# A graph layer and an LSTM on one core: residual additions moved to VectorE, the comparison moved ahead, preparation reordered

## The chip, the core and the metric

The kernel runs on one core of a Trainium2 chip. Its engines are TensorE (PE in the profile; its weight loads are PEld), VectorE (DVE), ScalarE (ACT), GpSimd (POOL) and SyncE (SP), which only issues transfers. The metric is the device time of one execution in microseconds. Three timed runs of the kernel took 1111.95, 1112.99 and 1113.43 us; the median is 1112.99.

## The reference

x has 1250 rows of 512 numbers; 20000 edges (src, dst) join rows, sorted by dst. Two residual layers follow each other:

```python
x = x + gnn(layernorm(x), src, dst, ...)
x = x + lstm(layernorm(x))          # one sequence of 1250 steps, state of 512
```

The graph part computes h = feat @ fc_w.T + fc_b, the degree of each row, and twice a sum over neighbours, a product with a 512x512 matrix w1, a product of h with a matrix w2, a bias and relu. The LSTM computes four gates from x_t and the state before, for 1250 steps, and its output h_t is added to x.

## The kernel before, in words

**Rows.** The 1250 rows are cut into P = 32 stretches of LEN = 40 rows. A tile has 128 rows (four of each stretch), and there are T = 10 tiles.

**Preparation** (lines 282 to 516). The edges are counted into a dense adjacency with matmuls: VectorE makes two one-hot matrices for each group of 125 edges (`make_onehot`, L401 and L403), PE multiplies them (L414, L417). Groups go in batches of four; 40 batches; eight buffers, so one-hots are made two batches ahead, and batch n + 2 is made when batch n has been multiplied. Beside that, for every tile t: `stats` (L153, L154) and `scales` (L158, L88 to L95, L339) give mean and scale of the first layer norm; `normed` (ACT, L429) normalises; `transposed` turns the tile on PE (L165) and copies it out on ACT (L170); `product` (PE, L176) multiplies by fcT; VectorE adds the bias (L488); the result is turned again, and two products with w2 follow, whose sums get their biases on VectorE (L463). fcT is made from fc_w by 16 transposes (`turn_fcw`, L377, copied out by L379). `with_identity` scales w2 on ACT (L181) and adds a diagonal on VectorE (L184).

The order on PE, VectorE and ACT is written out by hand (`manual_schedule`, L326): every engine runs its instructions in the order in which the program names them. A loop over slots s = 0 to 12 (L465) sets it. `per_slot` (L457) gives how many batches of edges are counted at three places of a slot, for s = 0, 1, 2, 3: (0,0,0), (1,1,0), (1,1,1), (1,2,1). In slot s, tile s is turned, tile s - 1 multiplied by fcT, h of tile s - 2 turned, and from slot 3 on tile s - 3 multiplied by the two w2. Statistics stand in slot 0 for tiles 1 to 3, in slot 1 for tiles 4 to 6, in slot 2 for tiles 7 to 9, each time right behind the turning of a tile; those of tile 0 stand ahead of the loop, inside the arithmetic on the edges (L383 to L389).

SP issues the loads, in this order: src, tile 0 of x (two transfers), fc_w as one transfer of 1 MiB (L300), tiles 1 to 3 (six), a bias, tiles 4 to 9 (eight), both w2, two biases, and ten fills with zeros of scratch space in HBM (L322). ACT issues dst and x's last rows. GpSimd makes the zeros (L320): 12 partitions of 6144 bf16 elements each.

**Graph layers** (L731 to L772): the sums over neighbours are matmuls with the adjacency (L750). The change doesn't touch them.

**LSTM** (`lstm`, L859). All 32 stretches run at once. Each starts WARM = 84 steps (and 12 more with fewer terms) ahead of its own rows, so that its state has settled by then; step n runs from -84 to 39, and steps 0 to 39 give output. Steps -84 to -63 also compute what the gates get from x. In a step, PE opens the gates from fetched data (L596) and adds 64 matmuls with the state (L604); then, for each half s, `cell` (L608) runs: ACT L611, L613, L615; VectorE L617, L618; ACT L620; VectorE L621, which writes hh (three buffers), and L622, which turns hh into the next state hT. In steps 0 to 39 GpSimd adds hh to the rows x2c (L1032), and after steps 7, 15, 23, 31, 37 and 39 `store` writes rows out. All stores but the last are issued by SP; the last has eight transfers, four on SP, two on ACT and two on GpSimd.

**Comparison.** `keep_state` copies the state before step 0 into snap (L890, L891) and the state after step 39 into last. If the warm-up was long enough, the end state of a stretch equals the state at the start of the next one. Five VectorE instructions and one matmul (L1039 to L1047) count the entries that differ; every engine loads the count (L1048), and if it isn't zero, a slow sequential version runs (L1050 to L1059).

Of the kernel before, what the change touches and what calls it, by code (L numbers as in the profile page):

```python
# [38 lines left out]
def gnn_lstm_kernel(  # L39
# [23 lines left out]
    nc = tc.nc  # L63
# [4 lines left out]
    R = 4 * P  # L68
# [91 lines left out]

    def transpose_in(ps, rows):

        p = ps.tile([128, KD, R], F32, name="psT")
        for k in range(KD):
            nc.tensor.transpose(p[:, k, :], rows[:, k * 128:(k + 1) * 128], ident)  # L165
        return p
# [37 lines left out]
    with ExitStack() as gnn_stack:  # L204
# [77 lines left out]
        with tc.tile_pool(name="prep", bufs=1) as prep, \  # L282
# [16 lines left out]
            fcw = prep.tile([128, KD, D], F32, name="fcw")  # L299
            nc.sync.dma_start(fcw, fc_w.rearrange("(a p) i -> p a i", p=128))  # L300
            biases = [prep.tile([R, D], F32, name=name) for name in ("fcb", "b1", "b2")]
# [16 lines left out]

            zeros = planes.rearrange("b t i d -> b (t i d)")[:4 * EARLY, :12 * G]
            nc.gpsimd.memset(zeros, 0.0)  # L320
            for v in xp_d:
                nc.sync.dma_start(  # L322
                    bass.AP(tensor=v.tensor, offset=v.offset,
                            ap=[[12 * G, 4 * EARLY], [1, 12 * G]]), zeros)

            with tc.manual_schedule(engines={mybir.EngineType.PE, mybir.EngineType.DVE,  # L326
# [6 lines left out]
                def stats(t0, t1):  # L333
                    for t in range(t0, t1):
                        layernorm_stats(work, mv, t, xt[:, t, :])

                def scales(t0, t1):
                    layernorm_scale(prep, mv[:, t0:t1, :], rstd[:, t0:t1], f"ln{t0}")
                    nc.vector.scalar_tensor_tensor(nmr[:, t0:t1], mv[:, t0:t1, 0], -1.0,  # L339
                                                   rstd[:, t0:t1], op0=OP.mult, op1=OP.mult)  # L340


                ends = []
                for name, rows in rows_i:
# [8 lines left out]
                    ends.append(e.rearrange("p i c -> p (i c)"))  # L353
                e_src, e_dst = ends
                none = edges.tile([ER, BW * T], F16, name="none")
                nc.vector.memset(none, 0.0)
# [14 lines left out]

                fcT = prep.tile([128, KD, D], F32, name="fcT")

                def turn_fcw(k):
                    p = psM.tile([128, D], F32, name="psM")
                    for a in range(KD):
                        nc.tensor.transpose(p[:, a * 128:(a + 1) * 128],  # L377
                                            fcw[:, a, k * 128:(k + 1) * 128], ident)
                    nc.scalar.copy(fcT[:, k, :], p)  # L379

                turn_fcw(0)
                turn_fcw(1)
                np_src, o_src = neg_floor_div(e_src, LEN, "stretch")  # L383
                stats(0, 1)
                scales(0, 1)
                turn_fcw(2)
                na_src, q_src = neg_floor_div(o_src, 4, "tile")
# [35 lines left out]

                xns, xTs, hTs, ps_h, ps_b = {}, {}, {}, {}, {}

                def normed(t):
                    if t < T:
                        xns[t] = work.tile([R, D], F32, name="xn")
                        nc.scalar.activation(xns[t], xt[:, t, :], AF.Identity,  # L429
                                             bias=nmr[:, t:t + 1], scale=rstd[:, t:t + 1])  # L430

                BATCH = 4
# [17 lines left out]

                normed(0)
                onehots(0)
                onehots(1)
                turn_fcw(3)

# [9 lines left out]
                for s in range(T + 3):  # L465
                    c0, c1, c2 = per_slot[s] if s < len(per_slot) else (0, 0, 0)
                    if 0 < s < 3:

                        ps_h[s - 1] = product(psM, xTs.pop(s - 1), fcT)
                        count(c0)  # L470
                    if s < T:
                        xTs[s] = transposed(work, psT, xns.pop(s), "xT")
                    if s < 3:
                        t0, t1 = ((1, 4), (4, 7), (7, T))[s]
                        stats(t0, t1)
                        scales(t0, t1)
                    normed(s + 1)
# [9 lines left out]
                    if 0 <= s - 1 < T:  # L487
                        nc.vector.tensor_add(h[:, s - 1, :], ps_h.pop(s - 1), fcb)  # L488
                    count(c2)
                    if s == 2:  # L490
                        for l in range(2):
                            with_identity(w2[l], ALPHA * betas[l], ALPHA * (1.0 - betas[l]))
# [335 lines left out]
        def store(x2c, n0, n1):  # L828

            def rows(j, p0, p1, m):  # L830
                (nc.sync, nc.scalar, nc.gpsimd, nc.sync)[j if n1 == LEN else 0].dma_start(
                    bass.AP(tensor=out.tensor, offset=out.offset + (LEN * p0 + n0) * D + 128 * j,
                            ap=[[LEN * D, p1 - p0], [D, m - n0], [1, 128]]),
                    x2c[32 * j + p0:32 * j + p1, n0:m, :])
# [24 lines left out]
        def lstm(first_yT, Wx, bx, Wh, wh_parts, close_wx):  # L859
# [6 lines left out]

            TOL = 2.0 ** -18
            first = -(WARM + BEFORE) % LEN // 4
# [6 lines left out]
            with ExitStack() as pools:  # L875
# [9 lines left out]
                    "b (n x y) -> b n x y", n=3, x=8)  # L885
                snap, last, apart = held[:, 0], held[:, 1], held[:, 2, :, :31]

                def keep_state(dst, hT):
# [87 lines left out]
                with tc.manual_schedule(engines={mybir.EngineType.PE, mybir.EngineType.DVE,  # L976
# [33 lines left out]
                    for n in range(-WARM, LEN):  # L1010
                        u = AHEAD + WARM + n
                        if n == 0:
                            keep_state(snap, hT)
                        if u == len(units):
                            load_x2c()
# [13 lines left out]
                        if u < len(units):  # L1029
                            put(u, 2)  # L1030
                        if n >= 0:
                            nc.gpsimd.tensor_add(x2c[:, n, :], x2c[:, n, :], hh)  # L1032
                            if n + 1 in stores:
                                store(x2c, ([0] + stores)[stores.index(n + 1)], n + 1)
                    keep_state(last, hT)

                nc.vector.tensor_sub(apart, last[:, :, 0:31], snap[:, :, 1:32])  # L1039
                nc.vector.scalar_tensor_tensor(apart, apart, -1.0, apart, op0=OP.mult, op1=OP.max)  # L1040
                nc.vector.tensor_scalar(apart, apart, TOL, None, OP.is_le)
                near = seq.tile([128, 1], F32, name="near")
                nc.vector.tensor_reduce(near, apart, mybir.AxisListType.XY, OP.add)
                pc = ps_c.tile([R, G], F32, name="pc")[:1, :1]
                nc.tensor.matmul(pc, near, ones, start=True, stop=True)
                far = seq.tile([1, 1], I32, name="far")
                nc.vector.tensor_scalar(far, pc, -1.0, float(128 * 8 * 31), OP.mult, OP.add)  # L1047
                n_far = nc.values_load(far, min_val=0, max_val=128 * 8 * 31)  # L1048
# [66 lines left out]
```

## Time and profile before

| what | us |
|---|---|
| median of three runs | 1112.99 |
| the profiled execution | 1113.26 |
| its span, first to last instruction | 1111.5 |
| PE busy in the span | 1007.0 |
| VectorE busy | 516.4 |
| ACT busy | 342.8 |
| GpSimd busy | 81.9 |
| start of the matmuls over neighbours (end of the preparation) | 195.2 |
| start of step 0 (first matmul of L604) | 917.3 |
| last state written | 1100.8 |

Times within the execution are counted from the start of the span. The profile's views used here are: the page; the chain of waits, which follows the work that ended last back through what released it; the timeline, which gives instructions in order of time with start, length, engine, line, names, shape and, in brackets, the idle time ahead and what ended it; and the table of stretches, which gives each engine's busy time and PE's granted clock (1.00 is full speed) in chosen intervals.

### The profile page before, as it was taken

The numbers are of one execution on the slowest core, as the hardware profiler recorded it, in microseconds if no ns is written. First come the engines' busy times: TensorE is split into PE (matmuls) and PEld (weight loads), VectorE is DVE, ScalarE is ACT, GpSimd is POOL, SyncE is SP. The second block draws the span as 40 slices with busy tenths as digits, with TensorE's granted clock in tenths as the row PEclk, the third lists the DMA queues.
The fourth block names the chain that finished last, engine by engine and source line by source line (L and its number), as shares of the span: only waits on it lengthen the run. The fifth ranks groups of instructions, "written<-read, shape, count | busy, mean of one in ns | idle before, by whom it ended". The sixth has DMA issues, their size and how long they took to land.

```text
span 1111.5 us, 26611 instructions
## 1 busy us (share of the span) xinstructions
PE 1007.0 (91%) x10972; PEld 517.7 (47%) x10972; DVE 516.4 (46%) x1753; ACT 342.8 (31%) x1267; POOL 81.9 (7%) x138
## 2 busy tenths in 40 slices
PE   4899999999999998999999988888888888888884
PEld 2455454554455443344444444444444444444442
DVE  7767667102400665655544544444444444444443
ACT  2322125203401024443333333333333333333332
POOL 2000000100000011111001170000000000011001
PEclk9899999999999999999999999999999999999998
DMA  7500000600200037662323393332233333334431
GB/s 217 79 1 1 1 1 35 234 1 18 74 1 1 0 113 230 205 184 82 109 85 114 101 231 97 97 90 87 88 89 99 88 88 87 107 77 116 119 78 20
DMA packets 37271, 98.51 MB, mean 89 GB/s; under 512 B 5711, under 2 KB 10680, under 8 KB 37018
## 3 DMA queue, kind: packets, MB, share of 16 engines
q1 hardware_dynamic: 27280, 68.67, 23.1%
q0 software_dynamic: 7232, 23.63, 6.2%
q10 hardware_dynamic: 2625, 4.39, 1.3%
q8 instruction: 89, 1.46, 0.5%
q14 instruction: 45, 0.36, 0.1%
HBM read 74.29 MB, written 19.76 MB: 85 GB/s over the span
## 4 chain that ended last, share of the span: by engine, by line
PE 49%; issue 26%; DVE 13%; ACT 7%; DMA 1%; SPq 1%; POOL 1%; DVEq 0%; ACTq 0%; POOLq 0%
PE gates L604 29%; PE psM L919 8%; PE psM L176 8%; DVE adj L617 3%; ACT adj L620 3%; DVE hT L622 2%; DVE cg L618 2%; DVE adj L621 2%; ACT cg L611 2%; PE acc L417 2%; ACT adj L613 2%; DVE od L403 1%; DMA fcw<-in_L_gnn_fc_w_dram 1%; POOL xp_d L939 1%; PE gates L596 1%
## 5 line engine op out<-in xcount | busy, mean ns | idle before, releaser
L604 PE MATMUL gates<-Wh,hT 128*32 128x256 f32 x7936 | 457.5, 381 | 61.4 <-DVE hT L622 61.3
L604 PEld LDWEIGHTS gates<-Wh,hT 128*32 128x32 f32 x7936 | 233.4, 109 | 257.1 <-DVE hT L622 122.9
L617 DVE TENSOR_TENSOR adj<-adj,cg 128x128 f32<-128x128 f32 x248 | 68.2, 275 | 231.7 <-ACT adj L613 231.5
L919 PE MATMUL psM<-Wx,xT 128*128 128x512 f32 x320 | 147.6, 607 | 0.5 <-DVE adj L929 0.5
L750 PE MATMUL agg<-adj,planes 128*128 128x512 bf16 x720 | 130.1, 344 | 1.9 <-DVE x L463 1.9
L611 ACT ACTIVATE cg<-gates 128x64 f32<-128x64 f32 x248 | 55.4, 224 | 213.6 <-PE gates L604 210.1
L620 ACT ACTIVATE adj<-cg 128x64 f32<-128x64 f32 x248 | 63.6, 256 | 131.7 <-DVE cg L618 131.7
L750 PEld LDWEIGHTS <-planes 128*128 128x128 bf16 x720 | 70.4, 98 | 62.4 <-DVE x L463 2.7
L621 DVE TENSOR_TENSOR adj<-adj 128x64 f32<-128x64 f32 x248 | 55.9, 225 | 82.5 <-ACT adj L620 82.5
L919 PEld LDWEIGHTS psM<-Wx,xT 128*128 128x128 f32 x320 | 58.7, 192 | 71.3 <-issue 69.0
L622 DVE STREAM_TRANSPOSE hT<-adj 128x64 f32<-128x64 f32 x248 | 60.9, 245 | 24.2 <-DVE adj L621 1.4
L613 ACT ACTIVATE adj<-gates 128x128 f32<-128x128 f32 x248 | 67.2, 271 | 0.1
L618 DVE TENSOR_TENSOR cg<-adj 128x64 f32<-128x64 f32 x248 | 55.8, 225 | 8.5
L939 POOL DMA_DIRECT2D xp_d<-planes x40 | 28.8, 719 | 408.4 <-issue 214.2
L176 PE MATMUL psM<-w,hT 128*128 128x512 f32 x128 | 58.6, 610 | 0.0
L615 ACT ACTIVATE adj<-gates 128x64 f32<-128x64 f32 x248 | 57.0, 230 | 0.0
L403 DVE TENSOR_SCALAR od<-ids,key 125x820 f16<-125x820 f16 (+42 forms) x160 | 55.6, 347 | 0.0
L596 PE MATMUL gates<-h,sel 96*32 96x256 bf16 x992 | 50.0, 273 | 0.0
L1032 POOL TENSOR_TENSOR base<-base,adj 128x128 f32<-128x128 f32 x40 | 18.4, 459 | 414.9 <-DVE adj L621 414.9
L417 PE MATMUL acc<-od,ob 125*128 125x400 f16 (+22 forms) x360 | 46.4, 259 | 0.4
L401 DVE TENSOR_SCALAR ob<-ids,low 125x128 f16<-125x128 f16 x160 | 39.6, 247 | 15.5 <-PE acc L417 15.4
L931 ACT CAST planes<-adj 128x512 bf16<-128x512 f32 x40 | 24.7, 618 | 60.8 <-DVE adj L929 60.7
(163 smaller groups left out, 722.3 us busy)
## 6 DMA issues: line engine op xcount, KB each, us to landing
h<-xp_d SPq DMA_DIRECT2D x136, 384.0 KB
xp_d<-planes POOLq DMA_DIRECT2D x40, 384.0 KB, 3.1
base<-x POOLq DMA_DIRECT2D x40, 64.0 KB, 4.5
w<-in_L_gnn_w_dram SPq DMA_DIRECT2D x2, 1024.0 KB
w<-in_L_gnn_w_dram POOLq DMA_DIRECT2D x2, 1024.0 KB, 5.9
xp_d<-planes SPq DMA_DIRECT2D x10, 144.0 KB
h<-in_x_dram SPq DMA_DIRECT2D x10, 128.0 KB
h<-in_x_dram SPq DMA_DIRECT2D x10, 120.0 KB
```

Source lines behind the costliest of these rows:

```text
L176: nc.tensor.matmul(p, lT[:, k, :], rhs[:, k, :], start=(k == 0), stop=(k == KD - 1))
L417: nc.tensor.matmul(blocks[i][:, (d0 - i * BW) * T:(d1 - i * BW) * T], ob, od[:, (d0 - lo) * T:(d1 - lo) * T], start=False, stop=last)
L604: nc.tensor.matmul(ps[s][32 * j:32 * (j + 1), :, :], hT[b // 2][:, b % 2, :], Wh[:, b, :, 128 * j + 64 * s:128 * j + 64 * (s + 1)], start= ...
L611: nc.scalar.activation(cg[:, 1, :], p[:, 3, :], AF.Tanh)
L613: nc.scalar.activation(sg, p[:, 0:2, :], AF.Sigmoid)
L617: nc.vector.tensor_mul(pr, sg, cg)
L618: nc.vector.tensor_add(cg[:, 0, :], pr[:, 0, :], pr[:, 1, :])
L620: nc.scalar.activation(th, cg[:, 0, :], AF.Tanh)
L621: nc.vector.tensor_mul(hh[:, m], so, th)
L622: nc.vector.transpose(hT.rearrange("p b c -> p (b c)"), hh[:, m])
L750: nc.tensor.matmul(p[:, :n * R], planes[:, k, pl, f * 128:(f + 1) * 128], adj[:, k, t0:t0 + n, :].rearrange("b i r -> b (i r)"), start=(k ...
L919: nc.tensor.matmul(p, yT[n][:, k, :], quarter(Wx[:, k, :, :], j), start=(k == 0), stop=(k == KD - 1))
```

## The change

It does six things:

1. The zeros in SBUF are 96 partitions of 768 elements instead of 12 of 6144. The HBM area filled is the same.
2. fc_w is loaded in four transfers of 128 rows, and `turn_fcw(a)` turns one such block instead of one block of columns.
3. The first tile's statistics, normalisation and turning, and the first two blocks of fc_w, stand ahead of the arithmetic on the edges; the other two blocks stand behind the first one-hots.
4. The statistics of tiles 4 to 6 move from slot 1 to the end of slot 2's counting, those of tiles 7 to 9 from slot 2 to slot 5.
5. The addition of hh moves from GpSimd to VectorE, behind the step's second cell. The last store's eight transfers are issued by SP and ACT in turn.
6. Both states are kept CHECK = 3 steps earlier (before step -3 and before step 37); the comparison runs on VectorE at the start of step 37, its matmul behind the cells of step 37. Where the count is loaded stays.

```diff
-    def transpose_in(ps, rows):
-        p = ps.tile([128, KD, R], F32, name="psT")
+    def transpose_in(ps, rows, name="psT"):
+        p = ps.tile([128, KD, R], F32, name=name)
...
-            nc.sync.dma_start(fcw, fc_w.rearrange("(a p) i -> p a i", p=128))
+            for a in range(KD):
+                nc.sync.dma_start(fcw[:, a, :], fc_w[a * 128:(a + 1) * 128, :])
...
-            zeros = planes.rearrange("b t i d -> b (t i d)")[:4 * EARLY, :12 * G]
+            W = 768
+            zeros = planes.rearrange("b t i d -> b (t i d)")[:4 * EARLY * 12 * G // W, :W]
             nc.gpsimd.memset(zeros, 0.0)
             for v in xp_d:
                 nc.sync.dma_start(
                     bass.AP(tensor=v.tensor, offset=v.offset,
-                            ap=[[12 * G, 4 * EARLY], [1, 12 * G]]), zeros)
+                            ap=[[W, 4 * EARLY * 12 * G // W], [1, W]]), zeros)
...
+                def turn_fcw(a):
+                    p = transpose_in(psM, fcw[:, a, :], "psM")
+                    nc.scalar.copy(fcT[:, :, a * 128:(a + 1) * 128], p)
...
                 e_src, e_dst = ends
+                stats(0, 1)
+                scales(0, 1)
+                turn_fcw(0)
+                normed(0)
+                turn_fcw(1)
+                xTs[0] = transposed(work, psT, xns.pop(0), "xT")
                 none = edges.tile([ER, BW * T], F16, name="none")
...
-                def turn_fcw(k):
-                    p = psM.tile([128, D], F32, name="psM")
-                    for a in range(KD):
-                        nc.tensor.transpose(p[:, a * 128:(a + 1) * 128],
-                                            fcw[:, a, k * 128:(k + 1) * 128], ident)
-                    nc.scalar.copy(fcT[:, k, :], p)
-                turn_fcw(0)
-                turn_fcw(1)
                 np_src, o_src = neg_floor_div(e_src, LEN, "stretch")
-                stats(0, 1)
-                scales(0, 1)
-                turn_fcw(2)
                 na_src, q_src = neg_floor_div(o_src, 4, "tile")
...
-                normed(0)
                 onehots(0)
                 onehots(1)
+                turn_fcw(2)
                 turn_fcw(3)
...
-                    if s < T:
+                    if 0 < s < T:
                         xTs[s] = transposed(work, psT, xns.pop(s), "xT")
-                    if s < 3:
-                        t0, t1 = ((1, 4), (4, 7), (7, T))[s]
-                        stats(t0, t1)
-                        scales(t0, t1)
+                    if s == 0:
+                        stats(1, 4)
+                        scales(1, 4)
                     normed(s + 1)
...
                     count(c2)
+                    if s in (2, 5):
+                        stats(s + 2, s + 5)
+                        scales(s + 2, s + 5)
                     if s == 2:
                         for l in range(2):
                             with_identity(w2[l], ALPHA * betas[l], ALPHA * (1.0 - betas[l]))
...
-                (nc.sync, nc.scalar, nc.gpsimd, nc.sync)[j if n1 == LEN else 0].dma_start(
+                (nc.scalar if n1 == LEN and j % 2 else nc.sync).dma_start(
...
-            TOL = 2.0 ** -18
+            TOL, CHECK = 2.0 ** -18, 3
...
+                def compare():
+                    nc.vector.tensor_sub(apart, last[:, :, 0:31], snap[:, :, 1:32])
+                    nc.vector.scalar_tensor_tensor(apart, apart, -1.0, apart,
+                                                   op0=OP.mult, op1=OP.max)
+                    nc.vector.tensor_scalar(apart, apart, TOL, None, OP.is_le)
+                    nc.vector.tensor_reduce(near, apart, mybir.AxisListType.XY, OP.add)
+
+                def count_apart():
+                    pc = ps_c.tile([R, G], F32, name="pc")[:1, :1]
+                    nc.tensor.matmul(pc, near, ones, start=True, stop=True)
+                    nc.vector.tensor_scalar(far, pc, -1.0, float(128 * 8 * 31), OP.mult, OP.add)
...
-                        if n == 0:
+                        if n == -CHECK:
                             keep_state(snap, hT)
+                        if n == LEN - CHECK:
+                            keep_state(last, hT)
+                            compare()
...
                         if u < len(units):
                             put(u, 2)
+                        if n == LEN - CHECK:
+                            count_apart()
                         if n >= 0:
-                            nc.gpsimd.tensor_add(x2c[:, n, :], x2c[:, n, :], hh)
+                            nc.vector.tensor_add(x2c[:, n, :], x2c[:, n, :], hh)
                             if n + 1 in stores:
                                 store(x2c, ([0] + stores)[stores.index(n + 1)], n + 1)
-                    keep_state(last, hT)
-                nc.vector.tensor_sub(apart, last[:, :, 0:31], snap[:, :, 1:32])
...
```

More of the change, by code (lines that the diff above doesn't have):

```diff
@@ L340, in scales, with normed @@
                                                    rstd[:, t0:t1], op0=OP.mult, op1=OP.mult)
+                xns, xTs, hTs, ps_h, ps_b = {}, {}, {}, {}, {}
+                def normed(t):
+                    if t < T:
+                        xns[t] = work.tile([R, D], F32, name="xn")
+                        nc.scalar.activation(xns[t], xt[:, t, :], AF.Identity,
+                                             bias=nmr[:, t:t + 1], scale=rstd[:, t:t + 1])
+                fcT = prep.tile([128, KD, D], F32, name="fcT")
+                def turn_fcw(a):
+                    p = transpose_in(psM, fcw[:, a, :], "psM")
+                    nc.scalar.copy(fcT[:, :, a * 128:(a + 1) * 128], p)
                 ends = []
@@ L370, in neg_floor_div @@
                     return q, r
-                fcT = prep.tile([128, KD, D], F32, name="fcT")
-                def turn_fcw(k):
-                    p = psM.tile([128, D], F32, name="psM")
-                    for a in range(KD):
-                        nc.tensor.transpose(p[:, a * 128:(a + 1) * 128],
-                                            fcw[:, a, k * 128:(k + 1) * 128], ident)
-                    nc.scalar.copy(fcT[:, k, :], p)
-                turn_fcw(0)
-                turn_fcw(1)
                 np_src, o_src = neg_floor_div(e_src, LEN, "stretch")
-                stats(0, 1)
-                scales(0, 1)
-                turn_fcw(2)
                 na_src, q_src = neg_floor_div(o_src, 4, "tile")
@@ L422, in count_group @@
                     return done
[L424 to L430, printed above, removed]
                 BATCH = 4
@@ L886, in lstm @@
                 snap, last, apart = held[:, 0], held[:, 1], held[:, 2, :, :31]
+                near = seq.tile([128, 1], F32, name="near")
+                far = seq.tile([1, 1], I32, name="far")
+                def compare():
[8 more added lines that the diff above has]
+                    nc.vector.tensor_scalar(far, pc, -1.0, float(128 * 8 * 31), OP.mult, OP.add)
                 def keep_state(dst, hT):
@@ L1030, in lstm @@
                             put(u, 2)
+                        if n == LEN - CHECK:
+                            count_apart()
                         if n >= 0:
-                            nc.gpsimd.tensor_add(x2c[:, n, :], x2c[:, n, :], hh)
+                            nc.vector.tensor_add(x2c[:, n, :], x2c[:, n, :], hh)
                             if n + 1 in stores:
                                 store(x2c, ([0] + stores)[stores.index(n + 1)], n + 1)
-                    keep_state(last, hT)
[L1039 to L1047, printed above, removed]
                 n_far = nc.values_load(far, min_val=0, max_val=128 * 8 * 31)
```

## The prediction

> **What bounds the kernel now.** I read the profile's own time first, then the chain of waits, then the timeline of its two ends. The profiled execution took 1113.26 us, its span 1111.5, so 1.8 lie outside the span; the three timed runs have their median at 1112.99, 0.3 lower. All sums below are made against 1113.3. The chain has three stretches that the change touches: the preparation (0 to 195 us), the 40 output steps (917 to 1101) and the tail (1101 to 1111.5).
>
> In the preparation the timeline shows VectorE held back at the start:
> ```profile
> 2.01 5.21 POOL L320 MEMSET planes<- 12x6144 bf16 x1
> 3.18 4.19 DVE L346 CAST src_f<-src_i 80x250 f32<-80x250 int32 x1 [2.29 <-DMA src_i<-in_src_dram]
> ...
> 8.46 0.28 DVE L346 CAST dst_f<-dst_i 80x250 f32<-80x250 int32 x1
> ```
> The two casts have one shape; the first takes 4.19 us, not 0.28, and ends at 7.37, just after GpSimd's memset (7.22). The table by stretches (columns: length, busy PE, PEld, DVE, ACT, POOL with counts, granted clock, DMA share, GB/s), cut where the clock changes, shows what PE does afterwards:
> ```profile
> 31.36:34.78 3.42, 1.09 (x8) 0.67 (x8) 3.32 (x13) 0.00 (x0) 0.00 (x0) 1.00 0.80 83
> 34.78:38.19 3.41, 1.99 (x9) 1.56 (x10) 2.93 (x17) 3.13 (x4) 0.00 (x0) 0.50 0.66 68
> 38.19:41.61 3.42, 3.42 (x5) 1.34 (x5) 3.42 (x20) 3.09 (x4) 0.00 (x0) 0.50 0.82 87
> 41.61:45.02 3.41, 3.35 (x26) 2.06 (x26) 2.60 (x16) 0.81 (x2) 0.00 (x0) 1.00 0.67 72
> ```
> VectorE is busy nearly throughout, PE waits for it, and after the idle stretch PE's clock is half for 6.8 us. From 45 to 100 us PE is then busy without a gap, and the chain follows it: a gain before 45 us is carried to the end, one behind it is not.
>
> In the output steps, the chain of waits at a step without GpSimd's add and at one with it:
> ```profile
> 911.88 0.27 ACT adj L620
> 912.15 0.03 issue
> 912.17 0.24 DVE adj L621
> ```
> ```profile
> 961.69 0.27 ACT adj L620
> 961.95 0.03 issue
> 961.98 0.02 DVEq L621
> 962.00 0.04 issue
> 962.05 0.24 DVE adj L621
> ```
> L621 writes hh. With the add, VectorE's queue takes one wait more in front of it, some 0.07 us, and that is the whole difference of the two steps.
>
> In the tail the chain is VectorE alone, and the store to HBM lies beside it (second fence, timeline):
> ```profile
> 1101.46 0.43 DVE S L1039
> 1101.89 0.02 issue
> 1101.91 0.43 DVE S L1040
> ...
> 1103.38 0.14 DVE far L1047
> ```
> ```profile
> 1101.02 1.72 SPq L831 DMA_DIRECT2D out_dram<-base  x4
> ```
> The last state is done at 1100.81, far at 1103.52, and the span ends at 1111.46: 7.9 us of register loads, barriers and one long GpSimd drain (4.56 us from 1106.06 in the instruction records).
>
> **Steps without GpSimd.** Step starts in the chain: 908.34, 912.80, 917.26 (4.46 apart), then 930.98, 935.51, 940.04 (4.53). The longer period begins at step 3, where the hh buffer read by GpSimd in step 0 is written again (three buffers). With the reader on VectorE that wait has nothing to wait for: 37 steps (3 to 39) by 0.07 is **-2.6 us**. From step 23 the period is 4.55 to 4.61, which I can't tie to the add; from 930.98 to 1094.98 the 36 steps take 164.0 us, at 4.46 they would take 160.6, so 3.4 is the upper end and 2.0 the lower. The add itself, 128x128 on two operands, has its like in L617 (0.275 us); it stands behind the step's last transpose, and VectorE is then idle 1.70 us before the next L617. That idle time hides it; without it, 40 additions would cost 12 us. Stores don't hold it: GpSimd's add of the step after a store (959.15) follows the one before (954.63) by 4.52, as elsewhere.
>
> **Comparison ahead.** Off the tail go two pairs of L890/L891 (1100.81 to 1101.43), L1039 to L1043, the matmul and L1047: 1100.81 to 1103.52, 2.7 us. They go to step 37, behind the add of step 36: add 0.28, states 0.62, comparison 1.64 (0.43, 0.43, 0.30, 0.42 and gaps) make 2.54 us in the 1.70 of idle time, so L617 and with it the step are late by **+0.85** (bounds 0.6 to 1.2). The first snapshot (0.62) fits its idle time at step -3 as it does at step 0. The one-column matmul stands on PE behind gates that are done, and far (0.14) behind the second cell: nothing. What is late in the tail then is the store. VectorE's add ends near 1101.1, SP issues four transfers in 1.72 us, ACT now four as well (its two took 0.38 and 0.70), to about 1103.0; load of the register and branch took SP 0.9 more. Against 1104.4 now that is 1103.9: **-0.5**. Unknown is GpSimd's drain. It has no stores any more (its two were issued up to 1102.4). If the drain belongs to them, all of it can go, and SP's own last waits (1106.8 now) set the end, up to 4.4 less. No other drain of the trace resembles it (0.19 us at the start). I take the drain as fixed, because it ends 8 us after the last of those issues while their median landing is 1.8 us, and keep 4.4 for the range.
>
> **Short fill.** 768 elements a partition for 6144: by proportion 0.65 us, between the 0.2 of a 128-element memset and the 5.21. Up to 1.17 us it is over before the cast starts (3.18). The cast then takes 0.28: 3.9 us earlier for VectorE's whole queue. The ten transfers of zeros stand last on SP and nothing waits for them until the 440s: nothing.
>
> **Order of the preparation.** VectorE ends dst_e at 9.87 now, at 6.0 afterwards. First statistics and scales run from 11.94 to 15.33 now, of which the square root spends 0.94 behind an fcT copy on ACT; it now stands ahead of those copies: 2.5 us, to 8.5. Then ids 0.58, divisions 1.51 and 2.11, one-hots of two batches 2.39, to 15.1, and statistics 1 to 3, 4.2 us, to 19.3, where 24.0 is now. Following that: xn 0.81, transpose 0.65, copy 0.59, second product at 21.5 (26.26 now), to 25.0.
>
> Here the second statistics (25.17 to 29.21 now) are gone, and what is late next is PE: batch 2 is counted after that product, and frees the one-hot buffers at 25.3. VectorE idles from 22.3, then makes one-hots 4 to 6 and a sum (4.5 us, to 29.8), and now does statistics 4 to 6 there (4.1, to 33.9). Their square root stands on ACT ahead of the scaling of both w2 (3.7 us, so 32.9 to 36.6), VectorE's diagonal additions end at 37.5, one-hots 7 and 8 at 38.9 and 40.3. PE has finished its third product and batch 6 at 32.3 and waits 5.5 us. So the first pair of w2 products starts at 40.5; the timeline has it at 45.15: -4.65. But PE's idle time now spans a full stretch of 3.4 us directly ahead of those products. The row above prices it: busy 32% of a stretch, the next at half clock. I take one half-clock stretch in front of full work, +1.7: **-3.0** net. Bounds: two stretches and a late third product, 0; no stretch, -5.
>
> The third statistics move from 32.33 to the end of slot 5. There 7.1 us of w2 products follow on PE without VectorE, and VectorE idles 2.6 and 2.1 us per slot waiting for PE; 4.1 us are covered, nothing. Were that cover gone, 4.1.
>
> **fc weight in four blocks.** Three issues more by 0.51 us on SP, 1.5 us for the rows and weights queued behind. The fifth row transfer now waits from 6.6 to 11.45 for the whole weight; with blocks that wait is for one block and should be no longer. A block's landing isn't shown; the nearest rows are x's first two transfers (124 KB each, issued 1.2 to 2.9, landed by about 5 by the bytes moved) and the whole weight (issued 2.99, landed 11.45). At either end the first product can start by 12.7 (weights 11.45, transposes, copy), and the second product waits for VectorE until 21.5: nothing, either way. The Trainium skill speaks against this part: DMA: Bandwidth & Descriptors, section Bandwidth, asks for transfers of 1 MiB and more, as smaller ones spend their time on fixed costs. By its 341 GB/s for 1 MiB the weight would be there in 3.1 us; the trace needed 8.5 beside the rows, and either way the first product isn't what VectorE's chain waits for.
>
> On the half clock: the Trainium skill's TensorE: Matmul & The Clock Gate, Part 1, says that an idle window of about 3.4 us halves the clock until a busy one has passed. Here windows of 32% and 39% sufficed (stretch from 14.3); by the rule read strictly a window would have to be empty, and the +1.7 might fall away.
>
> **Sum.** -3.0 - 2.6 + 0.85 - 0.5 = -5.25: **1108.0 us**.
>
> **Rivals.**
> 1. The drain goes with the stores: a further -4.4, 1103.6. For it: GpSimd then issues nothing behind the 650s. Against: 8 us between issue and end of the drain. 22%.
> 2. The front gives nothing: PE's 5.5 us of waiting in slot 3 cost two half-clock stretches and the third product falls into another. 1113.3 - 2.25 = 1111.0. For it: the statistics are put where no w2 products cover them. 15%.
> 3. The change doesn't remove the wait of the steps (VectorE needs one for its own reader): 1108.0 + 2.6 = 1110.6. Against: in the steps before 0, L622 reads hh on VectorE and there is no such wait. 4%.
> 4. Slower: the rows of x for tiles 1 to 3 land late. SP issues them behind three more transfers, and one of them waits for a block; VectorE, in order, stands still at statistics 1. I need them at 15.1. It decides from 22.6 on (7.5 us later eat the 5.25 and 0.2% of the time); landing at 26 gives 1119, at 23.5 about 1116. Against it: now they are issued by 13.2 in spite of the wait for the whole weight. 7%.
>
> The forecast's own case has 52%, 1105.5 to 1110.3.
>
> **Numbers.** A measurement tells about 0.2% (2.2 us) from no change. Faster by more: the forecast's case, rival 1, under half of 2 (6%), half of 3: 82%. Within: 11%. Slower: 7%. The range from 1101.5 (rival 1 with the steps at 3.4 and some of the front's 5) to 1111.5 (rival 2) leaves out rival 4, and some 5% on either side.
>
> **What would show it.** First cast near 0.28 us and statistics 1 to 3 ended near 19.3; first w2 product near 40.5 with a half-clock stretch about it; period 4.46 in steps 3 to 35 with no queue entry ahead of L621's like; step 37 longer by 0.85; from last state to end of span 10.1 us (10.65 now). The prediction fails if the drain shrinks, if PE reaches the w2 products later than 43, or if the steps keep 4.53.

## The result, and the profile after

Four runs of the changed kernel have their median at 1101.47 us (1100.31 to 1104.80), four of the kernel before at 1112.53. The ratio is 0.9905 (95% interval 0.988 to 0.9929): about 10.6 us are gone. The forecast was 1108.0, and its own case reached from 1105.5 to 1110.3; the median lies at the lower end of the whole range, 1101.5, which had been drawn for rival 1. The profiled execution of the changed kernel is the slowest of its four, 1104.80 us with a span of 1102.9; the stages below stand against the 1111.5 of before.

| stage, from the two traces (us) | before | after | difference | forecast |
|---|---|---|---|---|
| preparation, to the first matmul over neighbours | 195.21 | 192.96 | -2.25 | -3.0 |
| from there to step 0 | 722.05 | 722.62 | +0.57 | 0 |
| step 0 to the last state | 183.55 | 181.38 | -2.17 | -1.75 |
| tail, last state to end of span | 10.64 | 5.96 | -4.68 | -0.5 |
| sum | 1111.45 | 1102.92 | -8.53 | -5.25 |

The change doesn't touch the second stage. In the other traces of this document it takes 719.8 to 724.0 us, so its +0.57 is scatter. In the third stage, the trace of before has two single steps that take 0.35 us more than their neighbours (1 and 36), that of after has one (36); such steps stand at varying places in the other traces too, so 0.35 of the -2.17 isn't the change's.

**Front.** From the timeline of the kernel after (start, length, engine, line, names, shape, count, idle time ahead and what ended it):
```profile
2.01 0.73 POOL L323 MEMSET planes<- 96x768 bf16 x1
3.16 0.29 DVE L364 CAST src_f<-src_i 80x250 f32<-80x250 int32 x1 [2.28 <-DMA src_i<-in_src_dram]
...
12.76 3.70 PE L176 MATMUL psM<-fcT,xT 128*128 128x512 f32 x8 [0.68 <-ACT fcT L358]
...
20.17 1.11 PE L165 MATMUL psT<-ident,xn 128*128 128x128 f32 x4 [3.45 <-ACT xn L350]
...
21.96 5.63 PE L176 MATMUL psM<-fcT,xT 128*128 128x512 f32 x8 [0.56 <-ACT xT L170]
...
27.66 0.25 DVE L412 TENSOR_SCALAR ob<-ids,low 125x128 f16<-125x128 f16 x1 [4.37 <-PE acc L428]
...
35.03 3.69 ACT L181 ACTIVATE w<-w 128x2048 f32<-128x2048 f32 x2
...
40.05 1.38 PE L428 MATMUL acc<-od,ob 125*128 125x90 f16 x8 [5.49 <-DVE od L414]
...
42.84 8.79 PE L176 MATMUL psM<-w,hT 128*128 128x512 f32 x16
```
The cast has lost its 3.9 us. The second product starts at 21.96 (26.26 before) and the w2 products at 42.84 (45.15). The 5.49 us for which PE waits for a one-hot were forecast at 5.5. But the second product takes 5.63 us, not 3.70, and VectorE stands 4.37 us until PE has counted a batch behind it. The table of stretches says why (length, busy PE, PEld, DVE, ACT, POOL, granted clock, DMA share, GB/s):
```profile
15.64:19.05 3.41, 1.08 (x7) 0.34 (x5) 2.86 (x12) 0.20 (x1) 0.00 (x0) 1.00 0.97 225
19.05:22.46 3.41, 1.73 (x9) 1.55 (x10) 2.51 (x18) 1.96 (x3) 0.00 (x0) 0.50 0.99 275
22.46:25.88 3.42, 3.42 (x5) 1.33 (x4) 0.83 (x3) 0.16 (x1) 0.00 (x0) 0.50 1.00 359
...
36.12:39.53 3.41, 0.00 (x0) 0.00 (x0) 1.84 (x10) 3.41 (x4) 0.00 (x0) 1.00 0.00 0
39.53:42.95 3.42, 2.83 (x17) 2.42 (x18) 3.42 (x21) 1.46 (x3) 0.00 (x0) 0.50 0.00 0
```
There are two places of half clock: the forecast one at the w2 products (behind the empty stretch 36.12), and one more at the second product (behind a stretch with PE busy 1.08 of 3.41).

**Steps.** The chain of waits at an output step goes from ACT straight to VectorE; the queue entry ahead of L621's successor L627 is gone:
```profile
1090.40 0.27 ACT adj L626
1090.67 0.02 issue
1090.69 0.24 DVE adj L627
1090.93 0.02 issue
```
Steps 0 to 22 are 4.461 to 4.467 us apart, where steps 3 to 22 before were 4.525 to 4.530.

**Tail.** The chain's end, and then the store from the timeline:
```profile
1096.71 0.26 DVE hT L628
1096.97 0.15 DVEq L1064
1097.12 0.01 DVE base L1061
```
```profile
1097.16 1.70 SPq L837 DMA_DIRECT2D out_dram<-base  x4
1097.16 2.21 ACTq L837 DMA_DIRECT2D out_dram<-base  x4
```
The residual addition is the last work; eight issues follow, the last ends at 1099.37, and the span ends 3.5 us later. GpSimd's long drain (one of the records with which an engine ends) isn't behind that: in the instruction records it runs from 1090.47 to 1094.86, while the last step is still computed, and GpSimd then waits until 1102.14 for the others.

### The profile page after: what moved, and what is told of

Its sections match the earlier page's. It is cut to its first block, busy times and chain, and to the rows that moved or that the text cites. A ratio compares the mean times of both kernels' runs of the same rounds, so it can differ in the third digit from the quotient of the medians.

```text
span 1102.9 us, 26565 instructions
## 1 busy us (share of the span) xinstructions
PE 1006.7 (91%) x10956; PEld 518.5 (47%) x10972; DVE 520.3 (47%) x1793; ACT 343.7 (31%) x1267; POOL 57.9 (5%) x96
## 4 chain that ended last, share of the span: by engine, by line
PE 50%; issue 25%; DVE 13%; ACT 7%; DMA 2%; SPq 1%; POOL 1%; DVEq 0%; ACTq 0%; POOLq 0%
PE gates L610 29%; PE psM L942 8%; PE psM L176 8%; DVE adj L623 3%; ACT adj L626 3%; DVE hT L628 2%; DVE adj L627 2%; DVE cg L624 2%; ACT cg L617 2%; PE acc L428 2%; ACT adj L619 2%; DVE od L414 1%; POOL xp_d L962 1%; PE gates L602 1%; PE psT L165 1%
## 5 line engine op out<-in xcount | busy, mean ns | idle before, releaser
L756 PE MATMUL agg<-adj,planes 128*128 128x512 bf16 (+1 forms) x704 | 129.1, 343 | 2.7 <-DVE x L466 1.9
L627 DVE TENSOR_TENSOR adj<-adj 128x64 f32<-128x64 f32 x248 | 56.0, 226 | 80.4 <-ACT adj L626 80.4
L621 ACT ACTIVATE adj<-gates 128x64 f32<-128x64 f32 x248 | 57.3, 231 | 0.0
L412 DVE TENSOR_SCALAR ob<-ids,low 125x128 f16<-125x128 f16 x160 | 40.3, 252 | 18.6 <-PE acc L428 18.4
L602 PEld LDWEIGHTS <-sel 96*32 96x32 bf16 x992 | 26.6, 97 | 34.8 <-issue 15.9
```

Of the source, the lines that this page charges most:

```text
L602: nc.tensor.matmul(ps[s][32 * j:32 * (j + 1), :, :], lhs(j), rhs(j, s), start=True, stop=False)
L627: nc.vector.tensor_mul(hh[:, m], so, th)
L756: nc.tensor.matmul(p[:, :n * R], planes[:, k, pl, f * 128:(f + 1) * 128], adj[:, k, t0:t0 + n, :].rearrange("b i r -> b (i r)"), start=(k ...
```

## The experiments

Ratios are to the kernel before, run beside each experiment, so times of different experiments don't compare directly; the kernel after has 0.9905. A difference between two such ratios is uncertain by about 0.003, 3.4 us (half widths of 0.0025 and 0.0019, squared, added, rooted), so the stages of the traces have to carry the finer statements.

**1. Two transfers of the last store back on GpSimd** (kernel after otherwise).
```diff
-                (nc.scalar if n1 == LEN and j % 2 else nc.sync).dma_start(
+                (nc.sync, nc.scalar, nc.gpsimd, nc.sync)[j if n1 == LEN else 0].dma_start(
```


> The changed kernel with two of the last store's eight transfers back on GpSimd. Theory: GpSimd's drain has a fixed length of about 4.4 us and starts when GpSimd has nothing left to do; the change took it off the path only because GpSimd is done 9 us before the end. Then here it starts behind the two stores (about 1.7 us after the last state), and last state to end of span grows from 5.96 to about 8.8 us: some 2.8 us slower than the changed kernel. Rival: the tail got shorter because the comparison left it (2.7 us) and fewer engines' ends are waited for, and the drain doesn't matter: tail about 6.0, no difference.

Measured: 1105.11 us, 0.9946 (0.9927 to 0.9965); the tail is 10.52 us. The chain of waits now ends on GpSimd:
```profile
1093.64 0.51 POOL out_dram L837
1094.15 0.36 POOLq L1064
1094.52 0.20 POOL out_dram L837
```
The direction is the theory's, the tail is longer than its 8.8: between its last issue and the semaphore increase GpSimd waits 1.81 us (1095.03 to 1096.84) for semaphores, among them that of its second store, which the expectation hadn't counted.

**2. The comparison behind the last step again**, as before; stores and additions as after.
```diff
-                        if n == -CHECK:
+                        if n == 0:
                             keep_state(snap, hT)
-                        if n == LEN - CHECK:
-                            keep_state(last, hT)
-                            compare()
...
+                    keep_state(last, hT)
+                    compare()
+                    count_apart()
                 n_far = nc.values_load(far, ...)
```


> The changed kernel with both states kept and compared where they were before (state before step 0, comparison behind step 39); additions and stores without GpSimd as changed. Theory (drain of fixed length, starts when GpSimd knows the count and passes the branch): the tail is as in the kernel before, 10.6 us, step 37 gets back 0.6 us: 4.1 us slower than the changed kernel. Rival (the drain belonged to GpSimd's own stores and shrinks without them): tail 7.6 us, some 1.0 us slower.

Measured: 1104.31 us, 0.9929 (0.991 to 0.9948); the tail is 10.29 us (theory 10.6, rival 7.6) and step 37 takes 4.48.

**3. The additions on GpSimd again**; stores and comparison as after.
```diff
-                            nc.vector.tensor_add(x2c[:, n, :], x2c[:, n, :], hh)
+                            nc.gpsimd.tensor_add(x2c[:, n, :], x2c[:, n, :], hh)
```


> The changed kernel with the additions of hh back on GpSimd, nothing else. Theory: the period of steps 3 to 39 goes from 4.465 to 4.53 us (2.3 us in all) with a queue entry of VectorE ahead of the line that writes hh, and GpSimd's end starts behind the last addition, so the tail is about 7.5 us instead of 5.96: 3.8 us slower together. Rival (no drain on the path without GpSimd's stores): the period alone, 2.3 us slower with the tail at 6.0.

Measured: 1104.14 us, 0.9931 (0.9914 to 0.9949); the tail is 7.37 us (theory 7.5, rival 6.0), and the period is 4.52 to 4.53 in steps 4 to 22. The chain has its queue entry again:
```profile
1094.18 0.27 ACT adj L626
1094.44 0.03 issue
1094.47 0.02 DVEq L627
1094.49 0.04 issue
1094.53 0.24 DVE adj L627
```

What the three say of the tail stands in GpSimd's own instruction records, in us:

| kernel | GpSimd loads the count | its next long entry, a semaphore increase | its long drain | span ends | tail |
|---|---|---|---|---|---|
| before | 1103.56 | 1104.74 | 1106.06, 4.56 long | 1111.45 | 10.64 |
| 1, stores on GpSimd | 1094.11 | 1096.88 | 1098.30, 4.55 long | 1103.68 | 10.52 |
| 2, late comparison | 1097.66 | 1098.56 | 1099.94, 4.39 long | 1105.16 | 10.29 |
| 3, additions on GpSimd | 1096.13 | 1097.31 | 1098.60, 4.39 long | 1103.81 | 7.37 |
| after | 1088.20 | 1089.10 | 1090.47, 4.39 long | 1102.92 | 5.96 |

The drain is there in every kernel and has nearly one length, 4.39 us, or 4.55 where GpSimd issued stores at the end. What differs is its start: GpSimd goes into its end as soon as it has the count and nothing left to do. With the count late (2), or with work of its own at the end (the stores of 1, the last addition of 3), the drain lies behind the last state: each of these alone keeps the tail at 7.4 to 10.5 us. Without any of them it lies beside the last two steps. The other traces agree: the five kernels of experiments 6 to 10, which end as after does, have tails of 5.87 to 6.37 us, those of 4 and 5, which end as before does, of 10.64 and 10.65.

**4. The preparation of after with the LSTM and the tail of before.**


> The kernel before with the changes to the preparation alone (fill, fc weight, order, statistics); steps, comparison and stores as before. Theory (the two halves of the change add up; the changed kernel's profile shows 2.25 us less up to the matmuls over neighbours, and its median lies 3.3 us under its profiled execution, which I put down to half-clock stretches that fall differently): 2 to 5.5 us faster than the kernel before, and the first w2 products near 42.8 us in the profile. Rival: the preparation gives nothing that lasts (0 to 0.6 us, as the 0.55 left at the third product says), and the rest of the difference comes from the steps and the tail.

Measured: 1107.21 us, 0.9963 (0.9949 to 0.9977), so -4.1 us (-2.6 to -5.7). The matmuls over neighbours start at 193.15, the w2 products at 42.91 (expected 42.8), the tail is 10.64.

**5. The short fill alone** (kernel before otherwise).
```diff
-            zeros = planes.rearrange("b t i d -> b (t i d)")[:4 * EARLY, :12 * G]
+            W = 768
+            zeros = planes.rearrange("b t i d -> b (t i d)")[:4 * EARLY * 12 * G // W, :W]
...
-                            ap=[[12 * G, 4 * EARLY], [1, 12 * G]]), zeros)
+                            ap=[[W, 4 * EARLY * 12 * G // W], [1, W]]), zeros)
```


> The kernel before with the short fill of zeros alone. Theory (VectorE's queue binds up to 45 us, and the fill takes 3.9 us off its start): second product near 22.4 us instead of 26.3, first w2 products near 41 to 42 instead of 45.1, 3 to 4 us faster than the kernel before where the clock falls alike. Rival (the fc weight, landed at 11.45, or the rows of x take over): first product held near 13 to 15, at most 1.5 us of it lasts.

Measured: 1113.39 us, 0.9998 (0.9988 to 1.0008). It gives nothing, and the expectation of a gain fell; that the fc weight takes over was its rival (though the first product is at 18.46, not 13 to 15). The timeline of this kernel:
```profile
3.14 0.29 DVE L347 CAST src_f<-src_i 80x250 f32<-80x250 int32 x1 [2.25 <-DMA src_i<-in_src_dram]
...
12.37 3.76 PE L378 MATMUL psM<-ident,fcw 128*128 128x128 f32 x16 [6.80 <-DMA fcw<-in_L_gnn_fc_w_dram]
13.52 0.59 ACT L380 COPY fcT<-psM 128x512 f32<-128x512 f32 x1 [10.81 <-PE psM L378]
...
14.38 0.59 ACT L380 COPY fcT<-psM 128x512 f32<-128x512 f32 x1 [0.27 <-PE psM L378]
...
14.86 0.21 ACT L88 ACTIVATE ln_s<-ln_v 128x1 f32<-128x1 f32 x1
15.10 0.16 DVE L90 RECIPROCAL ln_r<-ln_s 128x1 f32<-128x1 f32 x1 [6.00 <-ACT ln_s L88]
```
VectorE is 3.9 us earlier up to the variance (9.1 us) and then stands 6.00 us at the reciprocal (1.18 before). Its square root is queued on ACT behind two copies of fcT, and those need the fc weight, for which PE waits until 12.37. So VectorE reaches the reciprocal at 15.10, where 14.21 was.

**6. The long fill in the kernel after.** The edit is that of 5, reversed.


> The kernel after with the fill of zeros as before: 12 partitions of 6144. The short fill alone gave nothing (0.9998), since VectorE, free 3.9 us earlier, then stood 6.0 us at the reciprocal L90: its square root is queued on ACT behind two fcT copies, which wait for the fc weight. Theory: fill and order are worth something only together. In the kernel after that square root stands ahead of the copies, so a long fill shifts VectorE's whole queue: first cast 4.2 us, statistics 1 to 3 ended at 23.1 (19.3 after), second product at about 25.4 (21.5 in the runs whose clock was full there), first w2 products near 46 to 47 (42.8), and the time is 3 to 5 us longer than after: 1104.5 to 1106.5. Rival: the order alone carries the gain and the shift is lost in the waits of VectorE and PE between 22 and 40 us (VectorE idle 4.4 us, PE 5.5): first w2 products within 1 us of 42.8, time 1101 to 1102.5.

Measured: 1107.29 us, 0.9937 (0.9924 to 0.995), 3.6 us (0.5 to 6.6 by the two intervals) over after. The second product and the first w2 products of its timeline:
```profile
25.41 3.70 PE L176 MATMUL psM<-fcT,xT 128*128 128x512 f32 x8 [0.58 <-ACT xT L170]
...
44.36 7.95 PE L176 MATMUL psM<-w,hT 128*128 128x512 f32 x16
```
The theory holds in its size; the w2 products lie 1.5 us later than in after, less than it said, since this execution has its clock at full at the second product. Against kernels with full clock there (1: second product 21.24, w2 products 40.19) they are 4.2 later each.

**7. The fc weight as one transfer** in the kernel after.
```diff
-            for a in range(KD):
-                nc.sync.dma_start(fcw[:, a, :], fc_w[a * 128:(a + 1) * 128, :])
+            nc.sync.dma_start(fcw, fc_w.rearrange("(a p) i -> p a i", p=128))
```


> The kernel after with the fc weight as one transfer. The whole weight lands near 11.5 to 12.4 us in the runs that load it so. Theory of the prediction: nothing either way. The four blocks are turned by 13.5 to 16, the first product moves from 12.76 to 16 to 18, but ends ahead of 21.5, where the second product waits for VectorE's statistics 1 to 3: first w2 products at 42 to 44, time within 1 us of after (1100.5 to 1102.5). Rival: the early blocks are what lets the new order work, since the turning of tile 0 and the first count stand behind the first blocks on PE and ACT: normalisation of tile 0, the first one-hots' count and with them VectorE's buffers come late, the second product goes to 25 or later, and the time is 3 to 5 us longer, 1104.5 to 1106.5.

Measured: 1102.30 us, 0.9905 (0.9888 to 0.9923), as after. Its timeline:
```profile
11.28 1.97 PE L165 MATMUL psM<-ident,fcw 128*128 128x128 f32 x8 [5.67 <-DMA fcw<-in_L_gnn_fc_w_dram]
...
17.28 3.70 PE L176 MATMUL psM<-fcT,xT 128*128 128x512 f32 x8 [0.67 <-ACT fcT L357]
...
22.41 3.70 PE L176 MATMUL psM<-fcT,xT 128*128 128x512 f32 x8 [0.58 <-ACT xT L170]
```
The first product moves by 4.5 us, the second by 0.45 against after; against kernel 1, which had full clock there as this one has, by 1.2, and so do the first w2 products (41.35 against 40.19). So the four blocks are worth some 1.2 us in these two traces, which the times (ratio difference 0.0, within 3.3 us) can't tell.

**8. The second and third statistics back in slots 1 and 2.**
```diff
-                    if s == 0:
-                        stats(1, 4)
-                        scales(1, 4)
+                    if s < 3:
+                        t0, t1 = ((1, 4), (4, 7), (7, T))[s]
+                        stats(t0, t1)
+                        scales(t0, t1)
...
-                    if s in (2, 5):
-                        stats(s + 2, s + 5)
-                        scales(s + 2, s + 5)
```


> The changed kernel with the second and third statistics where they were (slots 1 and 2). Theory: the second ones fit VectorE's idle time ahead of batch 2 and cost nothing, the third ones (4.1 us) stand where the second ones stand in the changed kernel, ahead of one-hots 5 to 7 and of the diagonals: first w2 products at 42 to 44 us, within 1.5 us of the changed kernel. Rival (keeping all eight microseconds of statistics out of the first slots is where the preparation's gain comes from): 4 us slower.

Measured: 1102.21 us, 0.9897 (0.988 to 0.9915). The two moves together, as they were made, are worth nothing that can be told (-0.9 us without them, within 3.4). The w2 products start at 43.34. What each move is worth, experiment 9 shows.

**9. The statistics of tiles 4 to 6 at the end of slot 1**, where VectorE waited 4.37 us, and not of slot 2.
```diff
-                    if s in (2, 5):
-                        stats(s + 2, s + 5)
-                        scales(s + 2, s + 5)
+                    if s in (1, 5):
+                        t0 = 4 if s == 1 else 7
+                        stats(t0, t0 + 3)
+                        scales(t0, t0 + 3)
```


> The changed kernel with the statistics of tiles 4 to 6 at the end of slot 1 instead of slot 2. Theory (PE's 5.5 us of waiting in slot 3 come from these 4 us of statistics standing where VectorE is late, while VectorE idles 4.4 us in front of batch 2): VectorE does them between 23 and 27 us for nothing, one-hots 7 come some 4.9 us earlier, the first w2 products start near 38 to 39 us instead of 42.8 and without a half-clock stretch over them: 4 to 6.6 us faster than the changed kernel, 1095 to 1097.5 us. Rival (what sets slot 3 is the second product at half clock, or the scaling of w2 on ACT): at most 1 us.

Measured: 1097.38 us, 0.9853 (0.9831 to 0.9875), 5.8 us (2.1 to 9.4 by the two intervals) below after. Timeline:
```profile
22.70 0.69 DVE L153 BATCH_NORM_STATS2 bnst<-base 128x6 f32<-128x512 f32 x1
...
27.22 1.17 PE L428 MATMUL acc<-od,ob 125*128 125x90 f16 x4 [0.88 <-DVE od L414]
...
27.50 3.72 ACT L181 ACTIVATE w<-w 128x2048 f32<-128x2048 f32 x2
...
35.91 7.04 PE L176 MATMUL psM<-w,hT 128*128 128x512 f32 x16
```
The statistics fill the wait, w2 is scaled 7.5 us earlier, and PE's 5.49 us of idle time are gone and with them the half clock at the w2 products, which start 6.9 us earlier. From 18.4 us, where the record of the clock begins, to 165 us the clock is full.

Not all of the 6.9 us is the move's: the moved statistics start at 22.70, behind the start of the second product (21.46), so that the clock was full at that product isn't their doing. Against experiment 1, whose clock was full there too, the w2 products start 4.3 us earlier and the fourth fc product, behind the half clock, 6.0 (43.86 against 49.90).

Kernels 8 and 9 differ in practice in the third statistics alone (slot 2 and slot 5), since the second ones start at 22.95 and 22.70 us. They lie 4.9 us apart (1.8 to 8.0 by the two intervals), their w2 products start at 43.34 and 35.91. So one set of statistics in slot 2, whichever it is, costs some 5 us; the change took the third set out of that place and put the second one in.

**10. Kernel 9 with the comparison dealt out**: keeping the state and the subtraction stand in step 37, the other three instructions and the matmul in step 38.
```diff
                         if n == LEN - CHECK:
                             keep_state(last, hT)
-                            compare()
+                            nc.vector.tensor_sub(apart, last[:, :, 0:31], snap[:, :, 1:32])
+                        if n == LEN - CHECK + 1:
+                            compare()
```


> The run before this one with the comparison dealt out to two steps: states and difference at the start of step 37, the rest at the start of step 38, its matmul behind that step. Theory (step 37 is 0.63 us longer because 2.5 us of VectorE's work stand in 1.5 to 1.7 us of idle time; GpSimd's drain, started 4.5 us later, is still over before SP's last waits): steps 37 and 38 at 4.47, 0.5 to 0.6 us faster, tail as in the changed kernel (6.0). Rival (the drain becomes the last thing to end): the 0.6 us come back in the tail, or more.

Measured: 1096.30 us, 0.9839 (0.9817 to 0.9861). Steps 37 and 38 take 4.479 and 4.483 us (5.086 and 4.392 in kernel 9). The two steps together are 0.52 us shorter, but the tail is 6.37 us against 6.06, so 0.3 us is left in the two traces from step 0 on. The longer tail isn't the drain, which ends at 1091.10 with GpSimd waiting until 1094.31. This version has the lowest median here; the two ratios can't tell it from kernel 9.

## Why the forecast was too high

**The step that failed is the tail's: "I take the drain as fixed, because it ends 8 us after the last of those issues".** The duration was right (4.56 before, 4.39 after), the place was not. The tail fell by 4.68 us where -0.5 was forecast. In the traces the whole difference to the forecast is 3.3 us (-8.53 against -5.25): the tail gives 4.2 more than forecast, the other stages together 0.9 less. Rival 1, which had 22%, had the number (a further -4.4) with half of its cause: the drain goes off the path, but not with the stores alone. The range held for that rival's sake and not by the forecast's own sum. Experiment 1 shows that stores on GpSimd suffice to keep it there, experiment 2 that a late count does so as well without any store. The prediction treated "comparison ahead" as 2.7 us of VectorE's time taken from the tail; what it was worth was that the one engine with a long end can start on it early. In the trace of before all five engines load the count within 0.01 us (1103.55 to 1103.56). That could be read as a common barrier. They only waited for the same number: in after GpSimd loads it at 1088.20, ACT at 1099.42.

**Steps: right.** -2.6 was forecast; 0.063 us a step were measured, 2.3 over 37 steps, and experiment 3 brings the queue entry and the longer period back. The still longer periods from step 23 on (the prediction read 4.55 to 4.61, the trace has 4.53 to 4.91) aren't the add's: without it, steps 23 to 25 take 4.54 us where they took 4.60 to 4.61, and step 33 takes 4.70 in both.

**Comparison on step 37: right in kind.** +0.85 was forecast; step 37 took 5.097 against 4.487 for its like and step 38 gave 0.10 back, +0.51. That it is VectorE's work in the idle time's place shows in the chain of waits of after, which runs through it:
```profile
1083.81 0.43 DVE S L900
1084.24 0.02 issue
1084.26 0.43 DVE S L901
1084.69 0.02 issue
1084.71 0.30 DVE S L903
1085.02 0.02 issue
1085.04 0.41 DVE near L904
1085.45 0.21 DVE adj L623
```
Experiment 10 takes it away by giving each of two steps what its idle time holds. The -1.8 that steps and comparison make together lies near the forecast's -1.75 because both terms were too large, which is luck.

**Front: right in size by the runs, by a sum with one term missing.** -3.0 was forecast, -4.1 (-5.7 to -2.6) is in the runs of experiment 4, -2.25 in the trace of after. In detail the list held where the clock was full: first cast 0.29, statistics 1 to 3 ended at 19.26 (19.3 forecast), PE's wait 5.49 (5.5). In experiment 1, whose clock was full at the second product, that product is at 21.24 (21.5) and the w2 products at 40.19 (40.5); the fourth fc product, behind the half-clock stretch that was priced, stands at 49.90 where 53.10 was: -3.2. The stretch ahead of the w2 products was empty (0.00 of 3.41 us), so the strict reading, by which the prediction's +1.7 might have fallen away, gives it too. In the trace of after the unforeseen half clock at 19.05 moves the w2 products to 42.84 and that mark to 52.55, -0.55. The other 1.7 us of its -2.25 are luck: the half-clock stretch that before had at 174.72 did not occur. The forecast named 43 as the point from which it fails; for this reason it came within 0.16 us of it.

Whether the clock is half at the second product goes with what it was before. Experiment 1, from its timeline, against the first PE lines of the fence of after:
```profile
12.79 5.48 PE L176 MATMUL psM<-fcT,xT 128*128 128x512 f32 x8 [0.68 <-ACT fcT L358]
...
19.91 0.66 PE L165 MATMUL psT<-ident,xn 128*128 128x128 f32 x4 [1.38 <-ACT xn L350]
...
21.24 3.70 PE L176 MATMUL psM<-fcT,xT 128*128 128x512 f32 x8 [0.58 <-ACT xT L170]
```
After and experiments 1, 2, 3, 4, 8, 9 and 10 run the same instructions up to there. In after and in 2 to 4 the record of the clock begins, at full, at 11.9 to 12.6 us; the first product takes 3.70 us, PE then stands idle for 3.44 or 3.45, and the half clock follows. In 1, 8, 9 and 10 the record begins at 16.3 to 18.4; the first product takes 5.40 to 6.51, the idle time shrinks to 0.64 to 1.69, and the half clock stays away there. The table of stretches shows 1.00 ahead of the record's first entry too, but nothing was recorded there; the length of the first product says that the clock was lower. The slow first product costs nothing that shows: the second starts at 21.24 to 21.55 in these four, at 21.78 to 21.99 in the other four.

The mean granted clock of the other three runs of after, 0.992 to 0.993 against 0.990, is higher by some 3 us of 1100, about what two half-clock stretches cost; whether they are the same two their runs don't tell.

**What the reasoning on the front didn't see** is that fill and order aren't two terms. The prediction gave the fill 3.9 us "for VectorE's whole queue" and the order 2.5 more. Alone, the fill gives 0.0 (5), and the order with the long fill loses 3.6 us of the gain (6), so that by subtraction 0.5 would be the order's alone; both together give the 4.1 of experiment 4. The wait behind the fcT copies was in the prediction's own text (0.94 us); it didn't ask how that wait grows when what stands ahead of it ends earlier.

**Blocks: nothing that the times can tell, as forecast** (7). The 3.1 us for the weight in the prediction is an estimate from a rate alone, and nothing rests on it; the trace had 8.5.

**Statistics: one move's gain paid for the other.** The prediction's PE wait of 5.5 us was real. By experiments 8 and 9 it was the cost of a set of statistics in slot 2, some 5 us; the prediction saw the third set leave and the second one come, and took the wait as given.

Rival 2 (the front gives nothing) isn't what the runs of experiment 4 show; in the profiled execution alone the front came near it up to the fourth fc product, by a half clock at the second product and not at the third. Rival 4 (rows late) didn't happen: VectorE's statistics 1 start at 15.04, as needed. Rival 3 is excluded by the chain of the steps.

Front -4.1 by the runs of experiment 4, and by the traces steps -2.3, comparison +0.5 and tail -4.7, make -10.6, as the ratio's 0.9905 of 1112.5 does. The front alone is uncertain by 1.6 us, so that they meet to a tenth is chance.

## What to carry to other kernels

Follow each engine to its own end: one with a long fixed end sets the time only if something holds it until the others are done, and both its own last work and a value that it waits for do so. When a stall is removed, ask what the same queue meets next and how that wait grows; two edits that each look like a gain can be one gain, or none. Before moving work out of a crowded place, look for a wait of the same engine in the trace that can take it: here the same 4 us of statistics cost nothing that shows in VectorE's wait in slot 1 and some 5 us one slot later. And compare variants in traces with the same clock, or a half clock that came and went is taken for the edit's.

## What the runs showed of the hardware

- GpSimd's end has a semaphore increase of 1.25 us and a drain of 4.39 us; with its own stores just ahead they take 1.29 and 4.55, and the increase starts 2.2 us after the last of those issues ended (1094.72 to 1096.88 in experiment 1), 1.81 of them in a wait for semaphores.
- One wait more in front of a VectorE instruction, for something done steps before, costs 0.06 to 0.07 us each time (period 4.53 against 4.465).
- Up to the tail the half clock comes in stretches of 3.41 us or whole multiples (6.83, 10.24), and where they begin differs between executions. No threshold of PE's busy time in the stretch ahead comes out of these traces. Stretches with 0.58, 0.75, 1.08, 1.52 and 1.71 us busy of 3.41 (experiments 4 and 5, after, 10 at 447 us, 6 at 456) were followed by half clock, and so was one with 2.21 (experiment 8, at 27 us). One with 1.51 (before, at 192 us) and those with 1.99 and 2.12 (experiments 10 and 1, at 16 us) were not. Twice the half clock followed a stretch with PE busy throughout (before at 174.72 us, experiment 9 at 165.18), which nothing here explains.
- The Trainium skill's TensorE: Matmul & The Clock Gate, Part 1, says that the window runs freely and asks for an idle one. The first agrees with stretches whose place shifts between executions; for the second, partly busy stretches, as listed, were followed by half clock here too.
